# A graph layer on one core: the edge search put first, x theta^T moved behind B, the list passes in a row, gathers that wait for maxima

## The chip, the cores and the metric

The kernel runs on one core of one Trainium2 chip. Five engines work side by side: TensorE (PE, with its weight loads PEld), VectorE (DVE), ScalarE (ACT), GpSimd (POOL) and SyncE (SP, which here only issues transfers). The metric is the device time of one execution in microseconds, the median of a few runs; a profile of one execution shows where it went.

## The reference

6250 nodes with 256 features, 100,000 edges sorted by their destination, two 256 × 256 weights:

```python
x_src = x[src]
x_dst = x[dst]
theta_x = (x_dst - x_src) @ theta_w.T + theta_b
phi_x = x_src @ phi_w.T + phi_b
e = jax.nn.relu(theta_x + phi_x)
out = jax.ops.segment_max(e, dst, num_segments=x.shape[0])
out = jnp.where(jnp.isfinite(out), out, 0.0)
x = _layernorm(x + out, axis=-1)
```

The sum inside relu is A[dst] + B[src], with A = x theta^T + bias and B = x (phi - theta)^T. A is the same for all edges of a node and relu is monotonic, so a node's result is relu(A + max of B over its edges). The work is one product for B, one for A, and a segmented maximum over 100,000 rows of B, fetched by source.

## The kernel before

**B.** x comes in shares of four 128-row tiles (`x_q`), is transposed on PE (`x_transposed`, L747), copied from PSUM by ACT, multiplied by phi - theta (`b_of`, L757) and stored to `b_rows` in memory. The gathers further down read `b_rows` and wait for the last of these stores.

**Two parts of the nodes, two ways to fetch.** Part 1 is the first 1130 nodes and their edges. Each of the 128 partitions takes 146 edges in a row; POOL gathers 128 rows of `b_rows` at a time, one edge of each partition (`gather`, L516, in groups of `STEPS` = 8 into a ring of six tiles named `g`), and DVE runs a maximum along each partition (`run`, L682): a step caps the row before, when its node is another, and takes the maximum. Every group's rows are stored to `maxima_1`; a node's result is later gathered from the place of its last edge. The first `X_GROUPS` = 2 groups are gathered from x itself, before B is there, and multiplied on PE in place (`x_group`).

Part 2 is the other 5120 nodes, 40 to each partition. For these the edges' rows are mostly fetched on PE. B is cut into 17 slots of 383 rows (three blocks of 128, less one row). For each node and slot, DVE chooses one edge whose source lies in the slot (`choice`, L990), and the chosen source number goes to memory, to be read back to all partitions (`want`). For each slot and chunk of 1024 nodes (`slot_part`, L1056) a mask with a one where a node wants a row (`hot`) is built by ACT in two passes for each block (Abs at L1067, Relu at L1068) or by DVE in one (L1065); PE multiplies the slot's rows, split in two terms, by the mask (L1075: 1960 products of 512 columns), and DVE takes the maximum into `acc` (L1086). Slot 0 is copied by ACT. The edges that were not chosen, 232 for each partition, form a list and go the way of part 1: gathered by `list_src` in 30 groups, run along each partition, stored to `maxima_2`, gathered by place.

**What stands ahead of it.** The kernel searches for the window of 800 edges in which a partition's nodes lie (`search_edges`, L622): the destinations' chunks are loaded to `dst_i`, cast, and two PE products (L634) give the counts. The windows are fetched from copies of the edges in memory (`dst_list`, `src_list`), since a branch behind the search (L653 to L662, a value loaded into all engines) sorts the edges there, if they are not in order, and searches again. With sorted edges it is not taken. `fill_table` (L931) then spreads the window's edges into a table of 40 × 36 places on DVE, in ten passes over 1440 columns, `choice` makes nine rounds on it, and `list_pieces` (L1167) packs what is left in eleven more passes, writes it to `list_words` and fetches it back in even chunks (`dst_w<-list_words`, three fetches on POOL).

**The order.** A planner puts the instructions on their engines; edges without a semaphore (`behind_in_order`, L503) fix the order where it matters, and POOL's instructions are in the order written (`in_turn`). The groups of the first part, slot parts and list passes are interleaved by hand (L1401 to L1453): a group after every second list pass, slot parts at one or two for each, then list groups with slot parts spread evenly over them (`SPREAD`).

**The end.** `rows_of` (L1273) loads x, gathers the maxima by place, transposes x again, multiplies by theta^T and adds the bias by a third product (L1292 to L1302), takes the maximum with the transposed `acc` for part 2 (L1309), adds, and `normalise` does the layer norm. `Shares` runs them one behind the other, part 1's eight full tiles first, then the 40 tiles of part 2. A last flag chooses a general path, not taken here.

Of the kernel before, what the change touches and what calls it, by code (L numbers as in the profile page):

```python
# [55 lines left out]
STEPS = 8  # L56
RING = 6
FIRST_STEPS = 146
X_GROUPS = 2
# [8 lines left out]
SPREAD = 0.97  # L68
# [7 lines left out]
X_RING = 5  # L76
# [351 lines left out]
def gnn_kernel(ctx: ExitStack, tc: tile.TileContext, x, src, dst, theta_w, theta_b, phi_w, phi_b, out):  # L428
# [34 lines left out]
    dst_list = dram.tile([EDGES], I32, name="dst_list")  # L463
    list_words = dram.tile([(P + 4) * OWN_LIST], I32, name="list_words")
# [36 lines left out]
    paced = [0]  # L501
# [14 lines left out]
    def gather(to, table, offsets):  # L516
        one = indirect(to, table, bass.IndirectOffsetOnAxis(ap=offsets, axis=0))
        for _ in range(paced[0]):
            in_turn(iota(pause, 1, 0, 0))
        return one  # L520
# [15 lines left out]
    def gather_group(i, table, a=0, b=STEPS):  # L536
        t0, n = groups[i]
        if i not in ring_tiles:
            ring_tiles[i] = gathered.tile([P, STEPS, D], FP, name="g")
        return [  # L540
            gather(ring_tiles[i][:, k, :], table, src_1[:, t0 + k : t0 + k + 1]) for k in range(a, min(b, n))
        ]

    gather_group(of_x[0], x, 0, EARLY_STEPS)


    dst_1 = const.tile([P, T1 + 2], I32, name="dst_1")
    early = body.enter_context(ExitStack())
    search = early.enter_context(tc.tile_pool(name="search", bufs=1))
# [5 lines left out]
    whole = [[E // P, P], [1, E // P]]  # L555
    rest = [[E % P, 1], [1, E % P]]
    pads = const.tile([P, 2, 8], I32, name="pads")
    nc.vector.memset(pads[:, 0, :], 0)
    nc.vector.memset(pads[:, 1, :], ID_MASK)
    for i, (to, edges) in enumerate(((dst_list, dst), (src_list, src))):  # L560
        nc.scalar.dma_start(flat(to, 0, whole), flat(edges, 0, whole))
        if E % P:
            nc.scalar.dma_start(flat(to, E - E % P, rest), flat(edges, E - E % P, rest))
        nc.scalar.dma_start(flat(to, E, [[8, P], [1, 8]]), pads[:, 1 - i, :])
    load_chunks(nc.scalar, dst_1, dst, T1, E)

    ident = const.tile([P, P], FP, name="ident")
    make_identity(nc, ident)
    ones = const.tile([P, 1], FP, name="ones")
    nc.vector.memset(ones, 1.0)  # L570
    flags = const.tile([1, 2], I32, name="flags")
# [14 lines left out]
    first_node = const.tile([P, 1], FP, name="first_node")  # L586
    iota(first_node, 0, N1, TILES)
    columns = const.tile([P, 3, P], FP, name="columns")
    iota(columns[:, 0, :], Q1, 0, 0)
    iota(columns[:, 1, :], 1, P * Q1, 0)  # L590
    iota(columns[:, 2, :], TILES, N1 - 1 + TILES, 0)
    lowest_rows = search.tile([P, 2 * D], FP, name="lowest_rows")
    nc.vector.memset(lowest_rows, LOWEST)
    nc.sync.dma_start(maxima_1[NONE_1 : NONE_1 + 1, :], lowest_rows[0:1, :D])
    nc.sync.dma_start(maxima_2[0:1, :], lowest_rows[0:1, :D])
    list_pads = search.tile([4, OWN_LIST], I32, name="list_pads")
    nc.vector.memset(list_pads, PAD_WORD)
    nc.sync.dma_start(flat(list_words, 0, [[OWN_LIST, 1], [1, OWN_LIST]]), list_pads[:1, :])
    nc.sync.dma_start(flat(list_words, (P + 1) * OWN_LIST, [[OWN_LIST, 3], [1, OWN_LIST]]), list_pads[:3, :])
    bad = const.tile([P, 9], FP, name="bad")  # L600

    descents = search.tile([P, T + 1], FP, name="descents")
    nc.vector.tensor_tensor(descents, dst_i[:, : T + 1], dst_i[:, 1:], op=ALU.is_gt)
    n_descents = search.tile([P, 1], FP, name="n_descents")
    nc.vector.tensor_reduce(n_descents, descents, AX.X, ALU.add)
    add_up(n_descents, flags[:, 0:1])

    ids = search.tile([P, T + 2], FP, name="ids")  # L610
# [10 lines left out]

    def search_edges():  # L622

        nc.vector.tensor_copy(ids[:, : T + 1], dst_i[:, 1:])
        iota(ids[:, T + 1 :], 0, 0, T)
# [3 lines left out]
        nc.vector.tensor_scalar(hot0, columns[:, 2, :], low0, None, op0=ALU.is_ge)  # L629
        nc.vector.scalar_tensor_tensor(hot0, columns[:, 2, :], ids[:, T : T + 1], hot0, op0=ALU.is_lt, op1=ALU.mult)  # L630
        cut = 2 * D
        for i, (a, b, n) in enumerate(((cut, T + 2, T), (0, cut, cut))):
            pp = misc()
            nc.tensor.matmul(pp[:, : b - a], hot0, ids[:, a:b], start=True, stop=True)  # L634
            nc.vector.tensor_scalar(
                descents[:, a:n], pp[:, : n - a], last_node, None, op0=ALU.is_le, op1=ALU.add, accum_out=counts[:, i : i + 1]
# [4 lines left out]
        nc.vector.tensor_scalar(window, counts[:, 0:1], float(E - WINDOW), None, op0=ALU.min)  # L641
# [7 lines left out]
    with (  # L649
        tc.tile_pool(name="sort", bufs=1) as sort,  # L650
        tc.tile_pool(name="ps_sort", bufs=2, space=PSUM) as ps_sort,
    ):
        n_unsorted = nc.values_load(flags[0:1, 0:1])  # L653
        with tc.If(n_unsorted > 0):
            sort_edges(nc, sort, ps_sort, src, dst, src_list, dst_list, ident)
            load_chunks(nc.sync, dst_i, dst_list, T, EDGES)
            load_chunks(nc.sync, dst_1, dst_list, T1, EDGES)
            load_rows(nc.scalar, src_1, src_list, P * T1)
            latest[0] = None
            gather_group(of_x[0], x)  # L660
            search_edges()
# [746 lines left out]
    for _ in range(2):  # L1408
        next_group_1(0)
# [88 lines left out]
```

## Time and profile before

| | us |
|---|---|
| median of 3 runs (723.31 to 733.8) | 727.39 |
| the profiled execution | 728.03 |
| its span, first to last instruction | 726.2 |
| PE busy | 623.0 |
| DVE busy | 623.9 |
| ACT busy | 485.5 |
| POOL busy | 486.0 |

A row of a group gives line, engine, operation, output and inputs with shapes, the count, busy time and mean length of one in ns, then the idle time of the engine just ahead of it and what ended most of that. "issue" means that the engine waited for nothing that the profile shows. A row of a timeline begins with its start and its length in us. A row of a window gives, after its bounds and length, the engines' busy time and counts, the granted TensorE clock, the share of the DMA engines and GB/s. The granted clock of this execution was 0.944 in the mean.

### The profile page before, as it was taken

The page shows a single profiled execution, that of the slowest core. Times are in us where ns is not written, and L with a number is a line of the kernel's source. Part 1 is how long each engine was busy: PE and PEld are TensorE (multiplying, and loading weights), DVE is VectorE, ACT ScalarE, POOL GpSimd, SP SyncE. Part 2 cuts the span into 40 slices and gives each one's busy share as a digit, 9 for nine tenths or more (in the row PEclk, how much of TensorE's full clock was granted, in tenths as well). Part 3 has the DMA queues.
Part 4 walks back from the last instruction along what each step waited for, and adds up shares of the span by engine and source line. Part 5 has one row for each costly group of instructions (what it writes and reads, how often), then busy time and mean ns, then how long its engine had stood idle before and what let it go on. Part 6 is the DMA issues. An engine that isn't in the chain of part 4 may idle for free.

```text
span 726.2 us, 9436 instructions
## 1 busy us (share of the span) xinstructions
PE 623.0 (86%) x2826; PEld 511.7 (70%) x2826; DVE 623.9 (86%) x1199; ACT 485.5 (67%) x676; POOL 486.0 (67%) x465
## 2 busy tenths in 40 slices
PE   0599895878987699999999999999999996699943
PEld 0388783646766587788888888888888884489942
DVE  6499999999977697986699999999999977878874
ACT  0144692899996475878777777777777771047882
POOL 6430057898877777777767577777777777757720
PEclk9799997999998799999999999999999998699976
DMA  8577335556677789986468788888888886745651
GB/s 223 147 261 242 138 106 171 183 166 203 187 224 232 252 260 366 336 279 176 146 206 280 251 284 280 269 281 281 272 286 275 257 261 225 244 139 191 225 200 71
DMA packets 56465, 164.77 MB, mean 227 GB/s; under 512 B 11899, under 2 KB 19860, under 8 KB 49332
## 3 DMA queue, kind: packets, MB, share of 16 engines
q1 hardware_dynamic: 32920, 98.76, 39.8%
q0 software_dynamic: 20944, 57.62, 27.2%
q10 hardware_dynamic: 2540, 7.69, 3.0%
q8 instruction: 25, 0.41, 0.2%
q14 instruction: 36, 0.29, 0.1%
HBM read 101.08 MB, written 63.74 MB: 227 GB/s over the span
## 4 chain that ended last, share of the span: by engine, by line
PE 55%; DVE 16%; DMA 12%; POOL 6%; issue 6%; ACT 3%; SPq 0%; DVEq 0%; POOLq 0%; ACTq 0%
PE ps_f L1075 45%; POOL g L513 6%; PE ps_e L1299 5%; DMA g<-b_rows,src 3%; DMA want<-chosen_rows 2%; DVE words L968 2%; DVE g L691 2%; DMA g<-b_rows,list_src 2%; DVE acc L1086 1%; PE ps_e L1292 1%; DVE work L965 1%; ACT hot L1067 1%; PE ps_e L1309 1%; DMA dst_w<-dst_list,window 1%; PE ps_b L764 1%
## 5 line engine op out<-in xcount | busy, mean ns | idle before, releaser
L1075 PE MATMUL ps_f<-hot,terms 128*128 128x512 f32 x1960 | 469.0, 400 | 33.2 <-DVE acc L1086 12.9
L1075 PEld LDWEIGHTS ps_f<-hot,terms 128*128 128x128 f32 x1960 | 376.4, 194 | 120.1 <-DVE acc L1086 15.1
L513 POOL DMA_INDIRECT g<-b_rows,list_src x232 | 235.8, 1016 | 73.5 <-issue 61.7
L1067 ACT ACTIVATE hot<-want,minus_row 128x1024 fp32r<-128x1024 f16 x176 | 193.9, 1149 | 95.6 <-PE ps_f L1075 80.4
L513 POOL DMA_INDIRECT g<-b_rows,src x130 | 168.0, 1292 | 92.4 <-DMA want<-chosen_rows 53.4
L1086 DVE TENSOR_TENSOR acc<-acc,ps_f 128x1024 f32<-128x1024 f32 x160 | 193.8, 1218 | 25.9 <-PE ps_f L1075 24.5
L691 DVE SCALAR_TENSOR_TENSOR g<-g,caps 128x256 f32<-128x256 f32 x376 | 181.7, 483 | 20.0 <-DMA g<-b_rows,src 12.3
L1068 ACT ACTIVATE hot<-hot 128x1024 fp32r<-128x1024 f32 x176 | 176.3, 1048 | 0.0
L513 POOL DMA_INDIRECT g<-maxima,place x49 | 47.3, 965 | 20.2 <-issue 13.7
L764 PE MATMUL ps_b<-weights,x_t 128*128 128x256 f32 x260 | 59.7, 384 | 0.7 <-ACT x_t L754 0.4
L1065 DVE TENSOR_SCALAR hot<-want,row_id 128x1024 fp32r<-128x1024 f16 x69 | 52.8, 766 | 7.2 <-DMA want<-chosen_rows 7.2
L764 PEld LDWEIGHTS ps_b<-weights,x_t 128*128 128x128 f32 x260 | 48.6, 192 | 8.4 <-ACT x_t L754 2.3
L1299 PE MATMUL ps_e<-weights,x_t 128*128 128x256 f32 x192 | 49.2, 385 | 0.2 <-ACT x_t L1294 0.2
L1299 PEld LDWEIGHTS ps_e<-weights,x_t 128*128 128x128 f32 x192 | 33.5, 194 | 3.8 <-ACT x_t L1294 0.5
L1329 ACT ACTIVATE squares<-x_f,r 128x256 bf16<-128x256 f32 x49 | 24.3, 500 | 17.0 <-DVE r L1326 17.0
L1294 ACT COPY x_t<-ps_e 128x512 f32<-128x512 f32 x24 | 13.7, 574 | 28.4 <-PE ps_e L1292 28.4
L767 ACT COPY b_sb<-ps_b 128x512 f32<-128x512 f32 (+1 forms) x25 | 14.5, 579 | 25.2 <-PE ps_b L764 25.2
L1344 ACT ACTIVATE x_f<-x_f,r 128x256 f32<-128x256 f32 x41 | 21.5, 591 | 9.9 <-DVE r L1336 9.9
L513 POOL DMA_INDIRECT g<-in_x_dram,src x16 | 19.7, 1232 | 9.5 <-issue 7.0
L1292 PE MATMUL ps_e<-ident,x_f 128*128 128x128 f32 x96 | 14.8, 280 | 11.6 <-DMA x_f<-in_x_dram 9.7
L1302 PE MATMUL ps_e<-bias_terms,pick 128*128 128x256 f32 x48 | 22.7, 473 | 0.0
L754 ACT COPY x_t<-ps_xt 128x512 f32<-128x512 f32 (+1 forms) x33 | 17.8, 593 | 6.2 <-PE ps_xt L752 6.0
(256 smaller groups left out, 435.0 us busy)
## 6 DMA issues: line engine op xcount, KB each, us to landing
maxima<-g SPq DMA_DIRECT2D x47, 1024.0 KB, 5.0
want<-chosen_rows SPq DMA_DIRECT2D x85, 256.0 KB, 4.8
x_q<-in_x_dram SPq DMA_DIRECT2D x12, 512.0 KB, 4.2
b_rows<-b_sb ACTq DMA_DIRECT2D x12, 512.0 KB, 3.5
raw<-b_rows SPq DMA_DIRECT2D x16, 256.0 KB, 4.4
x_f<-in_x_dram SPq DMA_DIRECT2D x4, 1024.0 KB, 8.9
out_dram<-x_f SPq DMA_DIRECT2D x4, 1024.0 KB, 4.4
g<-b_rows,list_src POOLq DMA_INDIRECT x232, 4.7
```

The source lines that it names most:

```text
L513: in_turn(nc.gpsimd.indirect_dma_start(out=out, out_offset=out_offset, in_=in_, in_offset=in_offset))
L691: one = nc.vector.scalar_tensor_tensor(g[:, k, :], last[part], caps[:, t : t + 1], g[:, k, :], op0=ALU.min, op1=ALU.max)
L764: nc.tensor.matmul(ps[:, h, :], x_t[:, h, k, :], weights[:, k, 0, :], start=(k == 0), stop=(k == KC - 1))
L1065: nc.vector.tensor_scalar(hot[:, b, :], want, row_id[:, b : b + 1], None, op0=ALU.is_equal)
L1067: nc.scalar.activation(hot[:, b, :], want, AF.Abs, bias=minus_row[:, b : b + 1], scale=1.0)
L1068: nc.scalar.activation(hot[:, b, :], hot[:, b, :].bitcast(FP), AF.Relu, bias=1.0, scale=-1.0)
L1075: nc.tensor.matmul(ps[:, w : w + 512], terms[:, part, b, h * P : (h + 1) * P], hot[:, b, w : w + 512], start=(i == 0), stop=(i == n - 1),)
L1086: latest_part[0] = nc.vector.tensor_tensor(to, to, ps, op=ALU.max).ins.name
L1292: nc.tensor.transpose(ps[:, 2 * i + c, :], x_f[:, k + i, c * P : (c + 1) * P], ident)
L1299: nc.tensor.matmul(a[:, i, :], x_t[:, 2 * i + c, :], weights[:, c, 1, :], start=(c == 0), stop=False)
L1302: nc.tensor.matmul(a[:, i, :], pick, bias_terms, start=False, stop=True)
L1329: nc.scalar.activation(squares, x_f[:, k, :], AF.Square, bias=mean[:, k : k + 1], scale=1.0, accum_out=var[:, k : k + 1])
```

## The change

- **Search first.** POOL makes the search's constants ahead of its first gathers; DVE goes from the cast to the search's mask and only then checks the edges' order; bias and pads move behind the first four loads of x (`bias_and_pads`). The windows are fetched from `dst` and `src` themselves. The copies and the branch are gone; unsorted edges are one more reason (`bad[:, 9:10]`) for the general path at the end, which sorts them first. Theta's copies and the first part's ids stand behind the window, B's transposes behind the search's products.
- **x theta^T behind B.** B's transposed x of part 2 is kept in `acc` (not in use yet); `a_columns` multiplies it by theta^T, with the bias, four tiles at a time, between the rounds of the choice, and stores it to `a_rows`. `rows_of` loads it back for part 2 (`a_f`) and does the old product for part 1 alone.
- **One group from x** (`X_GROUPS` 1), so 138 gathers of the first part read B.
- **List passes in a row**: fourteen pieces of `list_pieces` without groups between them. The steps of groups 1 to 5 come behind them on DVE. The gathers of six groups stand on POOL ahead of the list's fetch.
- **Held gathers**: from there on each second gather waits, with a semaphore, for the DVE step nine uses back (`used`); slot maxima stand behind the latest step of the first part (`strict`).
- **Slot parts** are spread over all groups from the list on, with the last 14 blocks left for the end, where each share's chunk is finished just ahead of it. DVE builds a block's mask in two parts of three; ACT's second pass covers all its blocks at once; `want` has three tiles.
- **Part 1's nodes** are finished during the list groups (from group 10 on), not behind them.

```diff
+AHEAD_OF_RUNS = 6
+TAIL_BLOCKS = 14
+EARLY_SHARES = 10
-X_GROUPS = 2
+X_GROUPS = 1
...
-    def gather(to, table, offsets):
-        one = indirect(to, table, bass.IndirectOffsetOnAxis(ap=offsets, axis=0))
...
+    def gather(to, table, offsets, k=None, further=0):
+        one = nc.gpsimd.indirect_dma_start(
+            out=to, out_offset=None, in_=table, in_offset=bass.IndirectOffsetOnAxis(ap=offsets, axis=0)
+        )
+        in_turn(one)
+        if held[0] and k is not None and k % 2 == 0:
+            after = mybir.DependencyInfo(mybir.DependencyClass.Sync, mybir.DependencyReason.DATA)
+            tc.add_manual_dep(one.ins, used[k - STEPS - 1 - further], after, reason="rows that are used")
+        return latest[0]
...
-        gather_run(dst_w, dst_list, window)
-        gather_run(src_w, src_list, window)
+        gather_run(dst_w, dst, window)
+        gather_run(src_w, src, window)
...
-        n_unsorted = nc.values_load(flags[0:1, 0:1])
-        with tc.If(n_unsorted > 0):
...
+            if column is None:
+                x_t = prep.tile([P, 2, KC, P], FP, name="x_t", bufs=3)[:, :w]
+            else:
+                x_t = acc[:, :, column * P : (column + w) * P].rearrange("p c (h n) -> p h c n", h=w)
...
+    def a_columns(j):
+
+        ps = ps_fetch.tile([P, CW], FP, name="ps_f").rearrange("p (i d) -> p i d", d=D)
+        for i in range(0, A_COLUMNS, 2):
+            nc.tensor.matmul(ps[:, i : i + 2, :], pick, bias_twice, start=True, stop=False)
+            for h in (i, i + 1):
+                at = (j + h) * P
+                for c in range(KC):
+                    nc.tensor.matmul(
+                        ps[:, h, :], acc[:, c, at : at + P], weights[:, c, 1, :], start=False, stop=(h == i + 1 and c == KC - 1)
+                    )
+        a_sb = a_tile.bitcast(FP)[:, j // A_COLUMNS % KB, :]
+        nc.scalar.copy(a_sb, ps.rearrange("p i d -> p (i d)"))
+        nc.sync.dma_start(flat(a_rows, j * D, [[TILES * D, P], [1, A_COLUMNS * D]]), a_sb)
...
-                nc.scalar.activation(hot[:, b, :], hot[:, b, :].bitcast(FP), AF.Relu, bias=1.0, scale=-1.0)
+        if of_dve < blocks:
+            apart = hot[:, of_dve:blocks, :]
+            nc.scalar.activation(apart, apart.bitcast(FP), AF.Relu, bias=1.0, scale=-1.0)
...
+                if strict[0]:
+                    behind_in_order(one, latest_run[0], "maxima ahead of the slots")
...
+    def fetch_parts():
+
+        groups_done[0] += 1
+        part_done = groups_done[0] / n_groups
+        while parts and blocks_left() - TAIL_BLOCKS > (all_blocks - TAIL_BLOCKS) * (1.0 - part_done):
             slot_part(*parts.pop(0))
+            dve_hots[0] = DVE_HOTS if len(parts) % 3 else 0
...
+        for j in a_todo[:1] if s0 else a_todo[:2]:
+            a_columns(j)
...
+    pieces = list_pieces()
+    for i in range(14):
+        next(pieces)
+        if i >= 14 - AHEAD_OF_RUNS:
+            gather_group(groups_1.pop(0), b_rows)
+        if i in (4, 7):
+            slot_part(*parts.pop(0))
+    for i in range(X_GROUPS, groups_1[0] - 1):
+        run_1(i)
     chunk_heads()
-    for i, _ in enumerate(list_pieces()):
-        if i == 14:
-            dve_hots[0] = DVE_HOTS
-            next_group_1(2)
-            next_group_1(2)
-        elif i % 2 == 0:
-            next_group_1(1)
-        else:
-            fetch_parts(1)
+    held[0] = True
+    next(pieces)
+    for i in range(3):
+        next_group_1()
...
+    for i, n in enumerate(widths):
+        j0 = sum(widths[:i])
+        while parts and parts[0] <= (NS - 1, (j0 + n - 1) * P // CW):
+            slot_part(*parts.pop(0))
+        at_end.add(2, j0, n)
```

More of the change, by code (lines that the diff above doesn't have):

```diff
@@ L67 @@
 DVE_HOTS = 1
-SPREAD = 0.97
 PAUSE = 160
@@ L910, in gnn_kernel @@
     )
-    iota(order, 1, 1, 0)
+    behind_in_order(iota(order, 1, 1, 0), windows_fetched[0], "runs ahead of the ranks")
     padded, unused = table("padded", I16), table("unused", I16)
@@ L956, in fill_table @@
         nc.vector.tensor_scalar(source, src_w, float(1 << 23), None, op0=ALU.add)
-        one = nc.vector.scalar_tensor_tensor(
+        nc.vector.scalar_tensor_tensor(
             words[:, TR - W :], distance, float(WORD), source, op0=ALU.mult, op1=ALU.add
         )
-        behind_in_order(nc.vector.memset(raw, LOWEST), one.ins.name, "edge table ahead of a slot's rows")
         going = work_2
@@ L1037, in slot_terms @@
         pieces = []
+        if s == 0:
+            behind_in_order(nc.vector.memset(raw, LOWEST), choice_end[0], "choice ahead of the slots")
         if whole:
@@ L1440, in gnn_kernel @@
         g_before = g
[L1441 to L1442 removed]
+        fetch_parts()
         if i >= LIST_GROUPS - 4:
```

318 lines of the change are left out of this document (183 added, 135 removed).

## The prediction

> **What bounds the kernel now.** I read the page first: the span, the chain of waits by engine, the groups of gathers. Then I counted the gathers in stretches of the run, because the chain names TensorE and the count does not.
>
> ```profile
> span 726.2 us, 9436 instructions
> ...
> PE 55%; DVE 16%; DMA 12%; POOL 6%; issue 6%; ACT 3%; SPq 0%; DVEq 0%; POOLq 0%; ACTq 0%
> ...
> L513 POOL DMA_INDIRECT g<-b_rows,list_src x232 | 235.8, 1016 | 73.5 <-issue 61.7
> L513 POOL DMA_INDIRECT g<-b_rows,src x130 | 168.0, 1292 | 92.4 <-DMA want<-chosen_rows 53.4
> L513 POOL DMA_INDIRECT g<-maxima,place x49 | 47.3, 965 | 20.2 <-issue 13.7
> ```
>
> The chain puts 55% on PE. But look at what GpSimd (POOL) did between gathers: the idle column says "issue" in nearly all of it, about 0.30 us before each. A gather of 128 rows costs 1016 + 300 ns there in the list part, 965 + 300 for the places. So POOL was hardly ever waiting for anybody: its queue of gathers is a second chain, as long as the first. The next view counts the gathers in stretches (columns: stretch, length, POOL busy and count).
>
> ```profile
> 97.00:125.00 28.00, 22.32 (x18) 0.85 0.45 132
> 125.00:152.00 27.00, 22.08 (x15) 0.97 0.67 222
> 152.00:200.00 48.00, 42.02 (x19) 1.00 0.54 168
> ...
> 232.00:310.00 78.00, 60.08 (x58) 0.91 0.87 297
> ...
> 360.00:600.00 240.00, 179.52 (x176) 1.00 0.83 265
> ```
>
> Late, 58 in 78 us is 1.34 us each and 176 in 240 us is 1.36. Early they are slow: 18 in 28 us (1.56), 15 in 27 (1.8), 19 in 48 (2.5). Two rows of the latest full stages, all engines (PE, PEld, DVE, ACT, POOL):
>
> ```profile
> 360.00:600.00 240.00, 240.00 (x1060) 198.48 (x1059) 225.80 (x345) 186.10 (x185) 179.52 (x176) 1.00 0.83 265
> ...
> 632.00:692.00 60.00, 57.90 (x359) 52.84 (x358) 49.19 (x151) 39.75 (x113) 41.60 (x44) 1.00 0.58 189
> ```
>
> From 360 to 600 PE is full (240 of 240 us), VectorE (DVE) 94%, and POOL 179.5 + 176 × 0.30 = 232 us of 240: PE and POOL end within 3% of each other. From 632 to 692 PE is full again with x theta^T, and POOL has only 44 gathers to issue in 60 us.
>
> **Step 1, an earlier B and an earlier window.** These rows are the start of the run.
>
> ```profile
> 9.33 0.56 DVE L624 CAST ids<-dst_i 128x783 f32<-128x783 int32 x1
> 17.73 2.95 PE L634 MATMUL ps<-ids,hot 128*128 128x272 f32 x4 [6.72 <-DVE hot L630]
> 21.90 0.15 DVE L641 TENSOR_SCALAR window<-counts 128x1 int32<-128x1 f32 x1
> 22.32 0.95 POOL L513 DMA_INDIRECT dst_w<-dst_list,window  x1 [6.89 <-DVE window L641]
> 25.76 1.51 PE L744 MATMUL ps_xt<-ident,w_in 128*128 128x128 f32 x6 [5.08 <-DVEq L654]
> 29.72 0.64 DVE L939 TENSOR_SCALAR wide<-dst_w,first_node 128x800 f32<-128x800 int32 x1 [3.58 <-DMA dst_w<-dst_list,window]
> 33.63 1.65 PE L764 MATMUL ps_b<-weights,x_t 128*128 128x256 f32 x5
> 71.77 0.73 DVE L997 TENSOR_SCALAR wide<-padded 128x960 int16<-128x960 int16 x2
> 97.50 0.96 POOL L513 DMA_INDIRECT g<-b_rows,src  x1 [53.37 <-DMA want<-chosen_rows]
> 125.13 1.65 DVE L1169 SCALAR_TENSOR_TENSOR wide<-padded,unused 128x1440 int16<-128x1440 int16 x1
> ```
>
> The search's products run at 17.73 although the ids were cast at 9.33; between them lie DVE's order check, the bias terms and the wait for them. Then the branch: PE's first transpose idles 5.08 us on it. In the changed order DVE goes straight from the cast to the search's mask, with the bias behind the weights. I take the cast 1 us earlier (the order check in front of it goes), the mask 1.3 us later, the products' 2.95 us and DVE's counts: window at 14 instead of 21.90. B no longer waits for a branch; it waits for the search's products and for theta's copies, which stand behind the window: first B product at 16 instead of 33.63, 17.6 us earlier. B stays on PE as before. So the first gather from B, 97.50, moves to 80. (Bounds: 75 if B runs cleaner without ACT's slot work in its midst; 88 if x's loads, now with bias and pads between them on SP, hold it back.) The dropped copies of src and dst cost only queue time on ACT and DMA; nothing else waits for them.
>
> The edge table starts when the window's rows are there: 29.72 becomes 14.3 + 7.4 = 21.7, since 22.32 to 29.72 is the time that this fetch takes. The choice (71.77) follows some 2 us closer, as the weights' and bias copies now lie ahead of the table: 61.8. The choice took 53.4 us to 125.13, with steps of the first part in it as now: it ends at about 114.
>
> **Step 2, the list in a row.** The work of the list on DVE, between 125 and 206 us, by line:
>
> ```profile
> L691 DVE SCALAR_TENSOR_TENSOR g<-g,caps 128x256 f32<-128x256 f32 x57 | 28.3, 497 | 0.0
> L1086 DVE TENSOR_TENSOR acc<-acc,ps_f 128x1024 f32<-128x1024 f32 x12 | 14.4, 1237 | 0.1
> ```
>
> Of 81 us, 28.3 are first-part steps and 14.4 slot maxima; some 4 more, in smaller groups, are node places and slots' terms. So the list by itself is 34 us, and in a row it ends at 148. POOL, however, must first get through the 48 gathers that stand ahead of the list's fetch (five groups and one; before there were 72). These rows show their price:
>
> ```profile
> 129.03 3.15 DVE L1172 TENSOR_TENSOR_SCAN work<-work 128x1440 f32<-128x1440 f32 x1
> 129.14 3.79 POOL L513 DMA_INDIRECT g<-b_rows,src  x1 [0.30 <-issue]
> ...
> 163.74 5.25 POOL L513 DMA_INDIRECT g<-b_rows,src  x1 [0.30 <-DVE g L691]
> ...
> 228.17 0.95 POOL L513 DMA_INDIRECT dst_w<-list_words,run_start  x1 [0.30 <-issue]
> ```
>
> A gather begun beside a scan of 3.15 us took 3.79, four times its normal length. With 1.56 us each until 114, 22 of 48 are done; at 2.5 us (the 152 to 200 row, the nearest to passes without a break) 14 by 148; the last 12 go at 1.34 beside the first part's steps: 164. The list's fetch, at 228.17 before, is then issued at about 164 to 168. Behind it stand gathers that are held: group 7's first waits for group 4's last maximum, and 32 steps at 0.483 us (0.6 with the small operations between) from 148 on end near 168. POOL resumes at 172 or so.
>
> [...]
>
> **Step 3, the queue from there to the list's end.** 90 gathers of the first part, 232 of the list, 3 for heads and carry, 9 for part 1's nodes: 334. The first part has 8 more gathers from B than before (X_GROUPS is 1), 10.5 us, while PE's 32 products less for them lie off the path. I take 1.32 us each, the list's mean 1.016 + 0.30, since PE will be less full than in the 1.36 stretch. 334 × 1.32 = 441 us: the list ends at 613; before, the same queue reached its part 1 gathers at 630.
>
> Do the other engines keep that pace? 231 of 245 blocks are spread over 42 groups, two parts apart: 5.36 blocks a group. The rows for the unit costs:
>
> ```profile
> L1075 PE MATMUL ps_f<-hot,terms 128*128 128x512 f32 x1960 | 469.0, 400 | 33.2 <-DVE acc L1086 12.9
> L1067 ACT ACTIVATE hot<-want,minus_row 128x1024 fp32r<-128x1024 f16 x176 | 193.9, 1149 | 95.6 <-PE ps_f L1075 80.4
> L1068 ACT ACTIVATE hot<-hot 128x1024 fp32r<-128x1024 f32 x176 | 176.3, 1048 | 0.0
> L1086 DVE TENSOR_TENSOR acc<-acc,ps_f 128x1024 f32<-128x1024 f32 x160 | 193.8, 1218 | 25.9 <-PE ps_f L1075 24.5
> L691 DVE SCALAR_TENSOR_TENSOR g<-g,caps 128x256 f32<-128x256 f32 x376 | 181.7, 483 | 20.0 <-DMA g<-b_rows,src 12.3
> L1065 DVE TENSOR_SCALAR hot<-want,row_id 128x1024 fp32r<-128x1024 f16 x69 | 52.8, 766 | 7.2 <-DMA want<-chosen_rows 7.2
> ```
>
> PE's 1060 records in 240 us (the row from 360) make 0.226 us each; 8 per block, 43 per group: 9.7 us. ACT builds the masks: with DVE's third of a mask 2 × 1.149 + one merged Relu of 2048 columns (2 × 1.048 less at most 0.1 us) = 4.3 us, without it 3 × 1.149 + 3.0 = 6.4, a mean of 5.0 for a part whose PE time is 5.4. With two mask tiles the 6.4 is not hidden in 5.4: about 1 us lost in three parts, 0.6 a group: 10.3. DVE: 8 × 0.483 + 1.79 parts × (2 × 1.218 + 0.67 × 0.766 + 0.2) = 9.5, overlaps not taken off. POOL: 8 × 1.32 = 10.6. All four lie within 10%, POOL last. The waits of the held gathers cost nothing when met: the gather at 163.74, released by DVE, shows the same 0.30 as the others. Part 1's nodes (9 tiles of x theta^T on PE, about 1.3 us each) add 12 us over twenty groups, 0.6 a group, which brings PE to POOL's pace and no further.
>
> x theta^T of the other 40 tiles moves ahead of the slots:
>
> ```profile
> L1299 PE MATMUL ps_e<-weights,x_t 128*128 128x256 f32 x192 | 49.2, 385 | 0.2 <-ACT x_t L1294 0.2
> ```
>
> 192 records took 49.2 us; 160 take 41. They start when B's last x group is done, a few us after the first gather from B, go in between the choices (PE waits there for each transposed choice) and end by 120, before slot 0 can start, whose terms stand behind the list's first passes. Cost nothing, hidden by DVE's choice and list; uncovered, PE would start the slots up to 41 us late, while it has 1728 × 0.226 = 390 us of blocks for 440 us. The ten stores and ten loads of it on SP, 512 KB each, pass beside the gathers.
>
> **Step 4, the end.** DVE's groups from 630 on, and two transfers:
>
> ```profile
> L1310 DVE TENSOR_TENSOR g<-g,ps_e 128x512 f32<-128x512 f32 x20 | 13.7, 687 | 8.1 <-PE ps_e L1309 7.9
> L1311 DVE TENSOR_TENSOR g<-g,ps_e 128x512 f32<-128x512 f32 x24 | 16.5, 686 | 3.1 <-PE ps_e L1302 2.7
> L1314 DVE SCALAR_TENSOR_TENSOR x_f<-g,x_f 128x256 f32<-128x256 f32 x48 | 18.5, 423 | 0.5
> ...
> maxima<-g SPq DMA_DIRECT2D x47, 1024.0 KB, 5.0
> ...
> g<-b_rows,list_src POOLq DMA_INDIRECT x232, 4.7
> ```
>
> From the last list gather (613) the chain is a landing (4.7), the last steps, a store (5.0), a place's gather and landing (4): first maximum of part 2 at 628. The 40 gathers at 1.27 would then end at 672. DVE has more: 13.7 for slot maxima, 13.7 for the sums (20 of 24), 16.9 for 40 of 48 steps, 3 for read-outs, 13 for the small operations of eight shares, 3 for shared scaling, and the tail's eight parts, 16 × 1.218 = 19.5, half of it in the 15 us wait: 73 us, less 5 for overlap. 628 + 68 = 696, where PE, without x theta^T, is no bound (14 blocks are 25 us). The last share's scaling and its store lie after DVE's last step, but so do some of the small operations counted here: one is taken for the other, span 697. Before it was 94 us from 632 to the end; now 84 from 613.
>
> Sum: span 697, with the 1.8 us between span (726.2) and its own time (728.03) 699; the median of the runs shown, 727.39, lies 0.6 below that: **698 us**, 4% faster.
>
> **Rivals.** *A slower one, the pipe coupled too tightly.* Before, six tiles of eight rows let POOL lead by some 40 gathers. Now each second gather waits for the maximum nine uses back, slot maxima stand strictly behind the first part's steps, and the masks of a part come ready together. If PE's waits for masks no longer fall into slack, the group's period is PE's with the waits added. At 10.9 us the list ends where it did (172 + 42 × 10.9 = 630); from 11.6 on the kernel is slower by 2%: 172 + 487 + 84 + 2 = 745. For it: four engines within 10%; ACT's 80 us of waits for PE before. Against: the hold leaves nine steps, about 12 us, and PE's blocks per group of eight gathers fall from 1060 / (8 × 22) = 6.0 to 5.4. Chance 0.08.
>
> *POOL starved by the list.* If no gather gets through the 34 us of passes, 26 are left at 148; at 1.34 they end at 183, the list's fetch is back at 187, the queue at 628, the end at 714. If DVE at the end is also at 90% rather than full, 722. Against: gathers did get through in 152 to 200. Chance 0.22, a third of it under 713.
>
> *A better one.* With DVE making a third fewer masks, gathers at 1.25 us (0.95 + 0.30, as most single rows show): 334 × 1.25 = 418, list's end 590; end 674. Chance 0.24.
>
> **Numbers.** My forecast (688 to 707) 0.46. Two percent is 14.5 us, about what a measurement of this kernel can tell: faster means below 712.8, slower above 741.9. Faster 0.46 + 0.24 + 0.08 = 0.78; within 0.14; slower 0.08. The range reaches into the better case and over most of the starved one: 668 to 724, with some 0.1 left out on each side.
>
> **What would show it.** Right: first gather from B near 80; list's fetch near 165; 1.32 us per gather until 613; PE with gaps between 180 and 600; x theta^T over by 120; DVE full from 628. Wrong: gathers idle on DVE rather than on issue (the coupled pipe), 5 us gathers between 114 and 150 (starved), PE or ACT the engine without gaps, or first B products after 22 us, where the search did not come first in fact.

## The result, and the profile after

| | us |
|---|---|
| before, median of 4 runs beside it (723.31 to 733.8) | 725.8 |
| after, median of 4 runs (746.58 to 751.17) | 748.5 |
| ratio, with its 95% interval | 1.030 (1.021 to 1.038) |
| after: the profiled execution, and its span | 748.03, 746.2 |

The changed kernel is 3% slower, where 698 us was forecast. In four later runs, two each of the kernels of experiments 13 and 14, every kernel, the one before the change too, took some 200 us longer (908 to 958 us, with single waits of up to 34.8 us that the profile of the first puts down to "remote"); the cause stayed open, and no figure here rests on them. The page of the changed kernel, span and chain of waits by engine:

```profile
span 746.2 us, 9108 instructions
...
PE 42%; DVE 20%; ACT 17%; DMA 11%; issue 7%; POOL 3%; SPq 0%; DVEq 0%; ACTq 0%; POOLq 0%
```

ScalarE (ACT) had 3% of the chain before; it has 17% now. That is a first sign that TensorE (PE) and ACT wait for each other. The timeline shows what the first two steps of the prediction spoke of (start, length in us, engine, operation, then the idle time ahead of it):

```profile
14.58 0.96 POOL L518 DMA_INDIRECT dst_w<-in_dst_dram,window  x1 [2.05 <-DVE ids L660]
16.65 5.38 PE L781 MATMUL ps_b<-weights,x_t 128*128 128x256 f32 x20
76.96 0.96 POOL L525 DMA_INDIRECT g<-b_rows,src  x1 [55.24 <-DMA b_rows<-b_sb]
...
166.95 1.07 POOL L518 DMA_INDIRECT dst_w<-list_words,run_start  x1 [0.30 <-issue]
...
176.63 1.08 POOL L525 DMA_INDIRECT g<-b_rows,src  x1 [5.22 <-DVE g L686]
```

The window's fetch (22.32 before), the first product of B (33.63), the first gather from B (97.50) and the list's fetch (228.17) all come earlier, by 8, 17, 21 and 61 us. POOL resumes with held gathers at 176.63. Not all of the 61 us is a lead, since 24 gathers that stood ahead of the list's fetch now stand behind it; the first gather by `list_src` goes at 295.67, before at 310.15. So some 15 us of lead were left there, and at the end the kernel is 20 us behind.

Where they went is read from stretches. First all engines (stretch, length, busy time and count of PE, weight loads, DVE, ACT and POOL, then the clock granted to PE), after and then before:

```profile
160.00:200.00 40.00, 23.46 (x86) 17.24 (x84) 33.81 (x100) 29.34 (x63) 26.62 (x29) 0.74 0.83 294
200.00:320.00 120.00, 100.48 (x397) 78.51 (x398) 86.67 (x145) 77.27 (x58) 92.42 (x93) 0.93 0.78 253
```

```profile
160.00:200.00 40.00, 33.92 (x143) 25.45 (x142) 39.87 (x57) 39.94 (x55) 34.82 (x18) 1.00 0.60 188
200.00:320.00 120.00, 104.08 (x414) 83.14 (x415) 97.51 (x192) 85.04 (x94) 92.99 (x94) 0.90 0.85 280
```

Between 160 and 200 us PE is busy for 23 us of 40, at a granted clock of 0.74 (before: 34 us, at 1.00). The longest single wait there, from PE's timeline, is for the terms of slot 1, which DVE makes only behind the first part's steps of groups 1 to 5:

```profile
201.18 4.21 PE L1118 MATMUL ps_f<-hot,terms 128*128 128x512 f32 x9 [8.72 <-DVE terms L1090]
```

Then the same windows for the slot products alone (PE, weight loads), where before was full; again after and before:

```profile
320.00:440.00 120.00, 112.76 (x489) 90.76 (x487) 1.00 0.71 224
...
640.00:680.00 40.00, 37.24 (x154) 27.92 (x152) 1.00 0.55 168
```

```profile
320.00:440.00 120.00, 119.85 (x528) 98.62 (x527) 1.00 0.72 229
```

489 products in 120 us against 528. PE is without work for 7.2 of the 120 us, in small pieces (the longest wait for a mask is 1.3 us), which is 32 of the 39 missing products at 0.227 us; the other 7 lie inside its busy time, where the ends of products are modelled. At 640 us, where before has none, 171 products are still to come (154 to 680, 17 behind). The list's last gather goes at 641.31, the last slot product at 698.8.

The groups of ACT's mask passes, with forms apart, and a third part in the steady stage:

```profile
L1108 ACT ACTIVATE hot<-want,minus_row 128x1024 fp32r<-128x1024 f16 x196 | 213.8, 1143 | 82.2 <-PE ps_f L1118 78.7 <-DMA a_rows<-hot 3.2
...
L1111 ACT ACTIVATE hot<-hot 128x2048 fp32r<-128x2048 f32 x49 | 93.9, 1916 | 1.0
L1111 ACT ACTIVATE hot<-hot 128x3072 fp32r<-128x3072 f32 x31 | 85.8, 2769 | 0.6
```

```profile
357.20 16.61 PE L1118 MATMUL ps_f<-hot,terms 128*128 128x512 f32 x72 [0.69 <-ACT hot L1111]
...
362.97 2.20 ACT L1108 ACTIVATE hot<-want,minus_row 128x1024 fp32r<-128x1024 f16 x2 [1.79 <-PE ps_f L1118]
364.51 0.74 DVE L1106 TENSOR_SCALAR hot<-want,row_id 128x1024 fp32r<-128x1024 f16 x1
365.21 1.92 ACT L1111 ACTIVATE hot<-hot 128x2048 fp32r<-128x2048 f32 x1
368.41 3.23 ACT L1108 ACTIVATE hot<-want,minus_row 128x1024 fp32r<-128x1024 f16 x3 [1.29 <-PE ps_f L1118]
...
371.55 0.82 ACT L1089 CAST terms<-raw 128x768 fp32r<-128x768 f32 x1
372.28 2.77 ACT L1111 ACTIVATE hot<-hot 128x3072 fp32r<-128x3072 f32 x1
375.10 16.61 PE L1118 MATMUL ps_f<-hot,terms 128*128 128x512 f32 x72 [1.28 <-ACT hot L1111]
```

At 362.97 a part with a block from DVE: two Abs, one Relu of two blocks, ready at 367.1. At 368.41 a part that ACT makes alone: three Abs (3.23), a cast of terms, a Relu of three blocks (2.77) that ends at 375.05. PE begins its products at 375.10, after 1.28 us without work, and then runs three parts (72 products) in 16.61 us. From the wait in 357.20 to that in 375.10 lie 17.9 us for three parts, where 72 products took 72 × 120 / 528 = 16.4 before. This is the longest such period here; the next three take 17.3 us each, 0.9 us more than before.

### The profile page after: what moved, and what is told of

Its sections match the earlier page's. It is cut to its first block, busy times and chain, and to the rows that moved or that the text cites. A ratio compares the mean times of both kernels' runs of the same rounds, so it can differ in the third digit from the quotient of the medians.

```text
span 746.2 us, 9108 instructions
## 1 busy us (share of the span) xinstructions
PE 622.4 (83%) x2672; PEld 501.1 (67%) x2672; DVE 612.0 (82%) x1176; ACT 515.9 (69%) x587; POOL 464.7 (62%) x465
## 4 chain that ended last, share of the span: by engine, by line
PE 42%; DVE 20%; ACT 17%; DMA 11%; issue 7%; POOL 3%; SPq 0%; DVEq 0%; ACTq 0%; POOLq 0%
PE ps_f L1118 36%; DMA g<-b_rows,src 8%; ACT hot L1108 7%; ACT hot L1111 7%; POOL g L525 3%; PE ps_f L822 2%; DVE words L1002 2%; DVE g L686 2%; DVE acc L1129 2%; DVE x_f L1383 1%; DVE g L1380 1%; DVE work L999 1%; PE ps L1358 1%; DVE wide L1035 1%; ACT acc L1127 1%
## 5 line engine op out<-in xcount | busy, mean ns | idle before, releaser
L1118 PE MATMUL ps_f<-hot,terms 128*128 128x512 f32 x1960 | 478.6, 404 | 52.3 <-ACT hot L1111 17.8
L1108 ACT ACTIVATE hot<-want,minus_row 128x1024 fp32r<-128x1024 f16 x196 | 213.8, 1143 | 82.2 <-PE ps_f L1118 78.7
L1111 ACT ACTIVATE hot<-hot 128x2048 fp32r<-128x2048 f32 (+2 forms) x85 | 185.0, 2177 | 1.8
L1106 DVE TENSOR_SCALAR hot<-want,row_id 128x1024 fp32r<-128x1024 f16 x49 | 37.1, 758 | 4.1 <-issue 2.0
L822 PE MATMUL ps_f<-weights,acc 128*128 128x256 f32 x160 | 37.8, 379 | 0.0
L781 PE MATMUL ps_b<-weights,acc 128*128 128x256 f32 x160 | 37.0, 383 | 0.2
L1369 PE MATMUL ps<-ident,acc 128*128 128x128 f32 x80 | 18.1, 366 | 19.6 <-DVE acc L1129 15.9
L822 PEld LDWEIGHTS ps_f<-weights,acc 128*128 128x128 f32 x160 | 30.4, 190 | 4.4
L781 PEld LDWEIGHTS ps_b<-weights,acc 128*128 128x128 f32 x160 | 29.6, 190 | 5.2 <-ACT acc L771 1.5
L1089 ACT CAST terms<-raw 128x768 fp32r<-128x768 f32 (+1 forms) x17 | 13.5, 794 | 21.9 <-DMA raw<-b_rows 21.9
L781 PE MATMUL ps_b<-weights,x_t 128*128 128x256 f32 x68 | 19.0, 440 | 0.1
```

Source lines behind the costliest of these rows:

```text
L781: nc.tensor.matmul(ps[:, h, :], x_t[:, h, k, :], weights[:, k, 0, :], start=(k == 0), stop=(k == KC - 1))
L822: nc.tensor.matmul(ps[:, h, :], acc[:, c, at : at + P], weights[:, c, 1, :], start=False, stop=(h == i + 1 and c == KC - 1))
L1106: nc.vector.tensor_scalar(hot[:, b, :], want, row_id[:, b : b + 1], None, op0=ALU.is_equal)
L1108: nc.scalar.activation(hot[:, b, :], want, AF.Abs, bias=minus_row[:, b : b + 1], scale=1.0)
L1111: nc.scalar.activation(apart, apart.bitcast(FP), AF.Relu, bias=1.0, scale=-1.0)
L1118: nc.tensor.matmul(ps[:, w : w + 512], terms[:, part, b, h * P : (h + 1) * P], hot[:, b, w : w + 512], start=(i == 0), stop=(i == n - 1),)
```

## The experiments

The theories for the 50 us between forecast and result: **masks** (the part that ACT makes alone is late, because with two mask tiles it can begin only when PE leaves the tile of two parts ago); **late start** (PE has fewer products done at 200 us, through x theta^T or through terms and maxima that stand on DVE behind the first part); **hold** (POOL's waits). Ratios are to the kernel before, run on the same chip.

**1. No hold.**

```diff
-    held[0] = True
```

> No gather is held for a maximum; all else as in the changed kernel. Three theories of why it takes 748 us. Hold: POOL's 43 us of waits for DVE's maxima put the list's end from the forecast 613 to 640; without them the list's gathers end before 620 and the time is 715 to 730. Late start: TensorE has 128 slot products done at 200 us against 257 before (129 x 0.226 = 29 us behind) and is the last to end; without the hold the gathers end earlier but the slot products do not, time 740 to 750. Masks: TensorE makes 160 to 169 products per 40 us where it made 178, because it waits for ACT's masks; time 740 to 750 here too.

747.4 us, ratio 1.033 (1.027 to 1.039): 1 us less, which lies within the spread of the runs. POOL's waits for DVE's maxima, first in the change and then here (engine, tile and line, what it waited for: us in total, times, longest):

```profile
POOL g L525 <- DVE g L686: 43.0, 48, 15.1
```

```profile
POOL g L525 <- DVE g L686: 2.6, 9, 0.3
...
POOL g L525 <- DMA want<-chosen_rows: 35.5, 1, 35.5
```

```profile
613.58 0.95 POOL L525 DMA_INDIRECT g<-b_rows,list_src  x1 [0.30 <-issue]
```

43 us of waits fall to 2.6, and 35.5 come back in one piece in front of the place gathers. The list's last gather, the last row, goes at 613.58, where 613 was forecast and the change has 641.31, and the time stays as it was. POOL was not the last to end: DVE makes the list's steps between slot maxima, which wait for PE 36 times between 320 and 640 us (36.9 us), and the last of these steps only at 644.45.

**2. Masks as before.**

```diff
-            dve_hots[0] = DVE_HOTS if len(parts) % 3 else 0
+            dve_hots[0] = DVE_HOTS
...
-        if of_dve < blocks:
-            apart = hot[:, of_dve:blocks, :]
-            nc.scalar.activation(apart, apart.bitcast(FP), AF.Relu, bias=1.0, scale=-1.0)
+                nc.scalar.activation(hot[:, b, :], hot[:, b, :].bitcast(FP), AF.Relu, bias=1.0, scale=-1.0)
```

> Masks built as before: DVE makes one block's mask in every part, and ACT's second pass is made block by block. Masks theory: 178 products per 40 us between 320 and 640 instead of 160 to 169, the slots end some 30 us earlier (1400 products x (0.250 - 0.225)), time 715 to 725. Late start: TensorE is as far behind at 200 us as now, 740 to 750. Hold: DVE has 55 more masks to build (0.77 us each), POOL's waits for its maxima grow, 745 to 760.

719.9 us, ratio 0.993 (0.989 to 0.996): a gain of 28.6 us, more than the whole loss against before. The slot products of this kernel in the same stretch:

```profile
320.00:440.00 120.00, 119.37 (x526) 98.23 (x525) 1.00 0.80 260
```

526 products, where before had 528.

**3. x theta^T left out.**

```diff
-            nc.tensor.matmul(ps[:, i : i + 2, :], pick, bias_twice, start=True, stop=False)
-            for h in (i, i + 1):
...
+            nc.tensor.matmul(ps[:, i : i + 2, :], pick, bias_twice, start=True, stop=True)
```

> The 160 products of x theta^T behind B are left out (the bias product, the copies and the stores stay), so that A of part 2 is only the bias in this kernel. Late start, in the form that these products stand in the way of the slots: TensorE is free of 41 us before 128 us and slot products begin up to 15 us earlier, time 725 to 735. Late start, in the form that slot 0's and slot 1's terms stand behind the list's passes and the first part's steps on DVE: the 41 us were idle time anyhow, 743 to 750. Hold and masks: 743 to 750.

748.2 us, ratio 1.034 (1.028 to 1.041). This kernel leaves out the products of A for part 2, so that A is the bias alone there. The 160 products cost nothing: they lie where PE had nothing else to do.

**4. Slot parts earlier.**

```diff
-        if i in (4, 7):
+        if i in (2, 4, 6, 8, 10, 12):
```

> Six slot parts instead of two stand between the list's passes, so that slot 0 is complete and slot 1's terms are made there and not behind the first part's steps of groups 1 to 5 (at 200 us now). Late start: TensorE has 180 to 200 products done at 200 us instead of 128, the slots end 12 to 16 us earlier, time 730 to 738. Masks and hold: the products gained early are lost in the same waits later, 743 to 752.

737.5 us, ratio 1.018 (1.012 to 1.024): a gain of 11, close to the 12 to 16 of the late start. PE's lag there is a loss of its own as long as PE is the last to end.

**5 and 6. Each half of the masks by itself**: Relu block by block, with DVE in two parts of three; then DVE in every part, with the Relu over both other blocks at once.

> Of the masks, only ACT's second pass is put back: one Relu for each block instead of one for all blocks of the part; DVE still builds a block in two parts of three. Theory of the wait: TensorE can start a part on its first block as soon as that block's mask is there, whereas the Relu of a whole part makes it wait 3 x 1.1 + 3.1 us; then this alone gives most of the 28 us that both edits gave, time 722 to 732. Theory of the load: ACT's sum, 6.4 us in each third part against 5.4 us of TensorE, is what limits, and splitting the Relu only adds starts of instructions; time 745 to 752.

> Of the masks, only DVE's share is put back: one block in every part; ACT's Relu covers the other two blocks in one instruction. Theory of the load: ACT then needs 2 x 1.15 + 2.2 = 4.5 us a part against 5.4 us of TensorE, the waits go, time 720 to 728. Theory of the wait: the part's second and third block still come ready together, a smaller loss stays in every part, time 732 to 742.

726.0 us (1.001, 0.999 to 1.004) and 720.0 us (0.993, 0.990 to 0.996). Their slot products, the Relu by blocks first:

```profile
320.00:440.00 120.00, 119.37 (x524) 98.20 (x525) 1.00 0.80 250
```

```profile
320.00:440.00 120.00, 119.37 (x525) 98.19 (x525) 1.00 0.83 264
```

Either half alone brings the rate back. DVE's block in every part also brings the whole gain; with the Relu by blocks 6 of the 28.6 us are still lost, and what they are was not tried. ACT's load in experiment 5 is higher than in the change (197.7 us of Relus block by block against 185.0), so load is not the cause of the lower rate. It is the pair: all three blocks on one engine and none of them ready before the last. In experiment 6 the part's two ACT blocks still come ready together, and it costs nothing, since 2 × 1.15 + 1.92 = 4.2 us fit into the 5.4 of a part.

**7. A third mask tile**, taken in turn with the two once the list's tables are gone; masks as in the change, but fewer x and A tiles for the end.

```diff
-X_RING = 4
-A_RING = 3
+X_RING = 3
+A_RING = 2
...
+        third_turn[0] += 1
+        if third and third_turn[0] % 3 == 2:
+            hot = third[0].tile([P, KB, CW], FR, name="hot_third")
+        else:
+            hot = slots.tile([P, KB, CW], FR, name="hot")
```

> The masks as in the changed kernel (merged Relu, DVE in two parts of three), but after the list's tables are gone a third mask tile is used in turn with the two; for its space the x tiles of the end are three instead of four and the A tiles two instead of three. Theory of the wait: ACT's mean of 5.0 us a part fits into TensorE's 5.4, and only the third part's 6.0 us in one piece (three Abs, 3.23, and a Relu of 2.77) is late because ACT can't begin it before the tile of two parts ago is free; with a third tile ACT works ahead, TensorE gets back to 176 to 179 products per 40 us between 320 and 440, time 718 to 726. Theory of the load: the whole sum of ACT's work is too large, or merged Relus disturb TensorE in another way; 160 to 168 products as now, time 743 to 752.

729.5 us, ratio 1.005 (1.003 to 1.008).

```profile
320.00:440.00 120.00, 119.37 (x519) 97.02 (x519) 1.00 0.77 247
```

519 products, most of the way from 489 to 526, with the same masks. The gain is 19 of the 28.6 us, a little short of what was expected; the smaller rings at the end were changed too, and what the other 9 us are was not tried.

**8. The kernel before with the change's masks alone** (the two edits of experiment 2 the other way round).

> The kernel before, with nothing of the change but its masks (Relu over all of ACT's blocks at once, DVE's block in two parts of three from the place where DVE began to make masks). If the mask scheme loses by itself wherever TensorE has no slack: its 178 products per 40 us fall to 160 to 166 from 320 on, some 25 us, time 745 to 755. If it loses only together with the held gathers, the later start or the strict order of the changed kernel: 722 to 732.

769.5 us, ratio 1.061 (1.055 to 1.067): 43.5 us lost, more than expected. The slot products, and PE's waits for DVE's maxima and for ACT's masks between 160 and 640 us:

```profile
320.00:440.00 120.00, 114.10 (x495) 92.43 (x496) 1.00 0.66 202
```

```profile
PE ps_f L1078 <- DVE acc L1089: 30.6, 5, 17.8
PE ps_f L1078 <- ACT hot L1071: 24.3, 25, 4.2
```

495 products instead of 528 and 24 us of waits for ACT's masks: the scheme loses by itself where PE has no slack, with no held gather and no late start. The waits for slot maxima, one of 17.8 us, are the part that was not expected, and that one is not the masks' own: until 612.85 DVE itself idles for 22.0 us, on the gathered maximum of a node of the share that is finished early, which stands ahead of the slot maximum on DVE (before, its longest wait for such a gather there was 3.9 us).

**9 to 12. Together: masks and early slots; also without hold; also without the strict order of slot maxima and terms; also with 6 blocks left for the end.**

```diff
-    strict = [True]
+    strict = [False]
...
-TAIL_BLOCKS = 14
+TAIL_BLOCKS = 6
```

> Masks as before, and six slot parts between the list's passes. If late start and masks are two separate losses, their gains add: 719.9 - (748.5 - 737.5) = 709, range 704 to 713. If, with the masks mended, POOL's queue or the landing of the list's last rows is the last to end (POOL's last list row is within some 10 us of the last slot product), the second edit gives less than half: 715 to 720.

> As the kernel before it in this list, with no gather held. If POOL is the last to end once TensorE is mended, the 25 us of waits for DVE's maxima now count, and this takes 695 to 705. If TensorE or DVE at the end decide, or the queue's lead slows others, no gain: within 4 us of the kernel with the hold.

> As the kernel with masks as before, early slot parts and no hold (711), but slot terms and slot maxima no longer stand behind the first part's steps on DVE. Late start: TensorE waits 12.3 us in one piece at 196 to 208 us for a slot maximum that DVE has behind 30 steps, and 3 to 4 us for terms; these go, time 695 to 702. If DVE's steps now come late instead, POOL waits for tiles and the list ends later: 708 to 715.

> As the kernel before it in this list, with 6 instead of 14 blocks left for the end. If the end is bound by TensorE's last blocks and DVE's waits for them (16 us of TensorE's waits for slot maxima lie there), 2 to 8 us faster than it; if the 8 blocks only move to a stage in which TensorE has no slack, they push the list's groups and it is 0 to 5 us slower.

717.9 (0.989, 0.985 to 0.994), 711.3 (0.981, 0.976 to 0.986), 710.9 (0.978, 0.973 to 0.982) and 707.3 us (0.974, 0.969 to 0.979). The early slots, worth 11 us alone, give 2 once the masks are mended, less than the spread of the runs; leaving out the strict order gives nothing, although its wait of 12 us was there. These two timelines of PE are of the kernel with the strict order and of the one without it:

```profile
208.50 10.77 PE L1116 MATMUL ps_f<-hot,terms 128*128 128x512 f32 x36 [12.29 <-DVE acc L1127]
```

```profile
211.41 19.23 PE L1116 MATMUL ps_f<-hot,terms 128*128 128x512 f32 x72 [7.31 <-DVE hot L1106]
```

The 12.29 us went, another wait of 7.31 came, and it did not matter which: the list's last gather is at 610.66 in the one and 610.85 in the other, and waits for nothing but its issue in both. Up to there POOL's queue now sets the pace: it takes 438 us for its 334 gathers, 1.31 each. The 3.5 us of the 6 blocks are not clear of the spread by themselves.

**13. Masks as before and no hold, nothing else.** The time is that of the second expectation's run, here and in experiment 14.

> Masks as before and no held gathers; slot parts as in the changed kernel. The prediction priced the hold at nothing; in the changed kernel leaving it out gained 1 us, with masks mended and slots early it gained 6.6. If the hold costs whenever TensorE is not the last to end, this takes 711 to 715 against 720 with the hold, and the list's last gather falls from 622.6 to 611. If the gain needed the early slot parts too, TensorE being last again without them: 717 to 722.

> The kernel with masks as before and no held gathers, a third time, hoping for a chip on which the kernel before takes its 726 us again. If the hold costs whenever TensorE is not the last to end: 711 to 715 against 720 with the hold, the list's last gather at 611 instead of 622.6. If the gain needed the early slot parts too: 717 to 722.

711.1 us, ratio 0.977 (0.970 to 0.984). Once the masks are mended the hold costs 8.8 us, by times of two chips; with the early slots it cost 6.6 on one (717.9 and 711.3). So the early slots are not needed for the gain. The list's last gather in the change, with masks mended, and with the hold gone too:

```profile
641.31 0.95 POOL L525 DMA_INDIRECT g<-b_rows,list_src  x1 [0.30 <-issue]
```

```profile
622.55 1.03 POOL L525 DMA_INDIRECT g<-b_rows,list_src  x1 [0.30 <-issue]
```

```profile
612.53 1.03 POOL L525 DMA_INDIRECT g<-b_rows,list_src  x1 [0.30 <-issue]
```

**14. No block left for the end.**

> As the kernel with 6 blocks left for the end (707), with none left. If the end is bound by DVE after POOL's last list gather (610 in all three), fewer slot maxima there gain again 2 to 3 us: 704 to 706. If the blocks now delay the list's last groups: 708 to 712.

> The kernel with no blocks left for the end, a third time. If the end is bound by DVE after POOL's last list gather: 704 to 706 against 707 with 6 blocks. If the blocks now delay the list's last groups: 708 to 712.

715.0 us, ratio 0.981 (0.974 to 0.989): 8 us slower than with 6 by the times, which are of two chips, 5 by the ratios, and above either expectation. The first place gather of the kernel with 6 blocks and of that with none:

```profile
621.84 0.95 POOL L525 DMA_INDIRECT g<-maxima,place  x1 [10.50 <-DMA maxima<-g]
```

```profile
632.02 0.94 POOL L525 DMA_INDIRECT g<-maxima,place  x1 [20.16 <-DMA maxima<-g]
```

The list's last gather is at 610.32 and 610.70, but DVE, with the last slots' masks and maxima between the list's last steps, makes the last of these (in which the first rows of the chunks are taken in) at 627.82 instead of 617.76, and all 40 place gathers wait for the store behind it:

```profile
617.76 0.42 DVE L684 TENSOR_TENSOR g<-g,heads 128x256 f32<-128x256 f32 x1
```

```profile
627.82 0.42 DVE L684 TENSOR_TENSOR g<-g,heads 128x256 f32<-128x256 f32 x1
```

## Why the prediction was wrong

**Step 1, right.** Window 14.58 (14 forecast), first product of B 16.65 (16), first gather from B 76.96 (80).

**Step 2, right.** The list's fetch is issued at 166.95 (164 to 168); POOL resumes at 176.63 rather than 172. Beside the list's passes 15 gathers got through between 113 and 155 us, where 14 were forecast to 148. The passes come in pairs, and one gather goes with each pair:

```profile
139.82 1.76 DVE L1249 COPY_PREDICATED work<-words,work 128x1424 int32<-128x1424 int32 x1
141.66 0.89 DVE L1246 TENSOR_SCALAR words<-work 128x1408 int32<-128x1408 int32 x1
142.72 1.73 DVE L1249 COPY_PREDICATED work<-words,work 128x1408 int32<-128x1408 int32 x1
```

```profile
140.13 2.54 POOL L525 DMA_INDIRECT g<-b_rows,src  x1 [0.31 <-issue]
142.97 2.56 POOL L525 DMA_INDIRECT g<-b_rows,src  x1 [0.30 <-issue]
```

The gathers start 2.84 us apart, a pair of passes takes 1.76 + 0.89 us and what lies between. These two gathers took 2.54 and 2.56 us, where the last of the list, at 641.31, took 0.95. But one gather still got through with each pair of passes, so the second rival, in which none does, did not come.

**Step 3, where it failed.** Its terms one by one. The queue: 334 gathers at 1.32, 441 us from 172 to 613. Without the hold it came so, whatever the masks: 171.35 to 612.53 with them mended (experiment 13), 171.60 to 613.58 with them as in the change (experiment 1). So the price was right. x theta^T hidden under choice and list: right (experiment 3), though it ended at 128 and not at 120. The masks: the step had "about 1 us lost in three parts, 0.6 a group", 25 us over 42 groups; the trace has 0.9 in most, and undoing them gained 28.6. The mechanism was seen and its size nearly so.

What failed is the balance, "all four lie within 10%, POOL last" (ACT, with its 1.79 × 5.0 = 9.0 us a group, lay 15% under POOL), with PE's "390 us of blocks for 440 us" as its cover. By the step's own numbers 390 + 25 for masks + 12 for the nodes of part 1 are 427: a slack of 13 us, never summed. Nor were the 390 the whole: 1728 products are 216 blocks, while its 5.36 blocks a group are 225 over 42 groups, 407 us, and 444 in all against POOL's 441. And it assumed that PE would work without a break from 172 us on. In the trace PE was busy for 23.46 + 100.48 of the 160 us from 160 to 320: 36 us without work, where before had 22, at a clock of 0.74 to 0.93. The waits in it for DVE's slot terms, slot maxima and masks are 8.7, 9.1 and 9.3 us. So PE and not POOL was the last, PE's waits counted, and POOL's earlier list bought nothing (experiment 1).

**The hold.** "The waits of the held gathers cost nothing when met" rested on one gather. They were not all met:

```profile
335.64 1.07 POOL L525 DMA_INDIRECT g<-b_rows,list_src  x1 [15.11 <-DVE g L686]
```

The steps of the list's first group stand on DVE behind slot maxima that wait for PE. That cost next to nothing while PE was last, and 7 to 9 us once it was not.

**Step 4.** 84 us from the list's last gather to the end. In the change it is 746.2 - 641.3 = 105, since 171 products and their maxima were still to come. In the best kernel it is 704.0 - 610.3 = 93.7, 10 us over the forecast. Before the change it was 98.7 from the list's last gather at 627.48; the step's 94 counts from 632, behind it. The first place gather goes at 621.84, in time for the first maximum forecast at 628, and the last at 673.7, where 672 was forecast. Between 630 and 690 DVE is busy for 49 of the 60 us, so it is not full. Its last step of a sum ends at 683.1, and 21 us of scaling and storing stand behind it: the forecast had set these against small operations counted twice, with a full DVE to 696.

**The rivals.** The slower one has the mechanism that came: "the masks of a part come ready together", waits of PE that "no longer fall into slack". That its 745 us lie so near 748.5 is partly luck: it had 11.6 us a group, the list's end at 659 and 84 us behind it, and measured were 11.1, 641 and 105. Its chance of 0.08 rested on the same unsummed slack. Four engines within 10% of each other, each with an idle time of its own ahead of it, were a reason for a much larger one.

Sum of what was shown: 748.5, less 28.6 (masks), less 8.8 (hold) is 711.1; early slots, no strict order and 6 blocks at the end bring 707.3, 2.6% below the kernel before. In spans 704.0 stands against the forecast 697: the list ends 3 us earlier than forecast, and the end is 10 us longer (step 4).

## What to carry to other kernels

Merging two passes over several blocks saves little on the engine that makes them (here 0.18 us for two blocks, 0.37 for three), but moves the time at which the first block is ready to the end of the last: with two buffers it is the longest single part that must fit into the consumer's time, not the mean (here 3.23 + 2.77 = 6.0 us against the 5.4 of a part on PE). When engines lie within some per cent of each other, add every term to each engine's own sum, from the moment at which it really can start, before any of them is called hidden. And a wait that costs next to nothing today may cost 9 us when the engine in front of it is mended, so take cuts back together as well as one by one.

## What the runs showed of the hardware

A Relu of three blocks took 2.77 us and one of two 1.92, against 3 × 1.05 and 2 × 1.05 block by block: 0.18 to 0.37 us saved, for a wait of PE of 0.7 to 1.3 us in three parts.

Between 160 and 200 us, with PE busy for 23 of 40 us, the granted clock was 0.74; before the change, with 34 of 40, it was 1.00. Between 200 and 320 us the order is the other way round: 0.93 with PE busy for 100 of 120 us, 0.90 before with 104. What the lower clock cost here was not measured apart.
